# Softmax sums of an attention: folded by transfers through HBM in place of ones-matmuls on TensorE, with the additions around them moved

## The chip, the cores and the metric

One core of a Trainium2 chip. The metric is the device time of one execution in microseconds (us), as the median of the runs on a chip; a kernel before and a kernel after are always timed on the same chip, in turn. No run of this case has to be set aside as a slow one: the runs of each kernel lie within 0.6% of each other. The granted clock, the share of its full clock that the chip let TensorE have, is given where it matters.

## The reference, cut to what matters

```python
# x: (8, 512, 32, 32); 8 images, 256 channels inside, 4 heads of 64 channels, 1024 positions
x = x + block(_gn(x), ...)            # _gn: group norm over each image

def block(x, ...):
    t = cbs(x, cv1_w, cv1_bn, 0)      # 1x1 convolution, batch norm, SiLU ("cv1")
    ys = [t[:, :C], t[:, C:]]
    for i in range(2):                # two attentions per image
        yi = ys[-1]
        z = cbs(yi, m_cv1_w[i], m_cv1_bn[i], 1)              # 3x3 convolution
        z = bot_attention(z, m_qkv_w[i], m_rw[i], m_rh[i])
        z = silu(bn_eval(conv2d(z, m_cv2_w[i], 0), m_cv2_bn[i]))
        ys.append(yi + z)
    return cbs(concatenate(ys), cv2_w, cv2_bn, 0)

def bot_attention(x, qkv_w, rw, rh):
    q, k, v = ...                     # 1x1 convolution
    r = rw + rh                       # position term, the same for every image
    a = softmax(einsum('bhdi,bhdj->bhij', q, k + r) * 64 ** -0.5)
    return einsum('bhij,bhdj->bhdi', a, v)
```

## The kernel before: the parts that matter

An attention runs in four groups; a group is two heads by 512 queries. In a group TensorE goes through four pairs of key blocks: it makes the logits (`l_ps`), ScalarE takes their exponential into `pt`, VectorE adds the exponentials up in `acc`, and TensorE multiplies them with v into `av_ps`, one pair later. At a group's end ScalarE and VectorE evict `av_ps` (copy it out of PSUM, the memory in which this kernel has TensorE's results) into `ao`. There is a single `av_ps` tile, so the product with v of the next group waits for this eviction. The sum over the 128 partitions of `acc`, the softmax's denominator, comes one group later, and two groups later `ao` is scaled by its reciprocal `rs`.

```python
def add_up(pair):                                   # VectorE: 1.22 us each
    g, j0 = pair[0]
    pt = pts[pair[0]]
    if j0 == 0:
        accs[g] = act.tile([P, 2, HALF], F32, tag="acc", name="acc", bufs=2)
        return nc.vector.tensor_tensor(accs[g], pt[:, 0], pt[:, 1], ALU.add)
    for i in range(PAIR):
        ins = nc.vector.tensor_tensor(accs[g], accs[g], pt[:, i], ALU.add)
    return ins

def times_v(pair):
    ...                                             # matmuls into avs[g]
    if j0 + PAIR == NJ:
        av = avs.pop(g)
        dst = ao[:, c, ts(half, HALF)]
        nc.scalar.copy(dst, av[:, 0])
        evicted[0] = nc.vector.tensor_tensor(dst, av[:, 1], dst, ALU.add)

def sums(g):                                        # the sum over partitions, on TensorE
    NQ4 = HALF // 2
    ps = ps_big.tile([P, NQ4], F32, tag="big", name="s_ps")
    acc = accs.pop(g)
    for at_q in range(4):
        hd, part = divmod(at_q, 2)
        nc.tensor.matmul(ps[at_q * 32 : (at_q + 1) * 32, :], ones[:, 0:32],
                         acc[:, hd, ts(part, NQ4)], start=True, stop=True,
                         tile_position=(0, at_q * 32))
    ...                                             # ScalarE copies it, SP stores 4 rows to HBM

def spread(g, s_dram):                              # load them as 128x8, invert, spread again
    nc.vector.reciprocal(rc, total(g, s_dram))
    nc.sync.dma_start(r_dram.rearrange("h (i r) -> (h i) r", r=QP), rc)
    ...                                             # two loads that repeat a row give rs

for i in range(len(pairs) + 1):
    if i < len(pairs):
        added = logits(pairs[i])                    # l_ps, exponential, add_up
        g, at_q = divmod(i, NQ)                     # NQ = 4 pairs in a group
        with tc.issue_after(added.ins):
            if at_q == NQ - 2 and g > 0:            # behind the third pair's additions
                rss[g - 1] = spread(g - 1, s_drams[g - 1])
            if i == 1 and later is not None:
                later()                             # adds r to the second half of k
            if at_q == 1 and g > 1:
                scale(g - 2, rss.pop(g - 2))
    if i > 0:
        g, j0 = pairs[i - 1][0]
        if j0 == 0 and g > 0:
            s_drams[g - 1] = sums(g - 1)
        times_v(pairs[i - 1])
        ...
```

Other work is placed behind the attention's pairs: in the first attention of an image, the next image's group norm (`x<-x,gm,gr`, where `gr` is a small power on GpSimd) and the operands `t_x` of the next image's cv1, a Strassen product (fewer matrix products, for more additions before and after them); in the second, cv1's last additions and its own. The products of cv1 stand around the end of the first attention:

```python
def begin():
    for c in range(2):                              # VectorE: the operands t_x
        tt(t1[:, c], b12[c], b11[c], ALU.subtract)
        ...
    kept["ps"] = product(a11, b11)                  # x_ps; needs no t_x
    kept["m1"] = to(spare("xr", 2), kept["ps"])
    to(y0_2, product(s4, b22))                      # nor does this one
def rest():
    kept["m5"] = to(spare("xr", 2), product(s1, t1))
    ...
```

Of the kernel before, what the change touches and what calls it, by code (L numbers as in the profile page):

```python
# [59 lines left out]
def kernel(  # L62
# [170 lines left out]
    def make_sq(n, tag, bufs):  # L233
        (a11, a12), (a21, a22) = ([block_qkv(n, o, i) for i in range(2)] for o in range(2))
        parts = [act.tile([P, 2, 3, P], F32, tag=tag, name="sq_new", bufs=bufs) for _ in range(2)]
        s1, s2, s3, s4 = (t[:, j] for t in parts for j in range(2))
        nc.vector.tensor_tensor(s1, a21, a22, ALU.add)
        nc.vector.tensor_tensor(s2, s1, a11, ALU.subtract)
        nc.vector.tensor_tensor(s3, a11, a21, ALU.subtract)
        nc.vector.tensor_tensor(s4, a12, s2, ALU.subtract)  # L240
        for h, t in enumerate(parts):
            nc.gpsimd.dma_start(sq_dram[n][:, 2 * h : 2 * h + 2], t)

    def load_sq(n):
# [119 lines left out]
    def stages(act, small, ps_big, ps_av, n_pt):  # L364
# [245 lines left out]

        def project_strassen(n, z, sq, t):

# [90 lines left out]
            def later():  # L703
                for half in range(NH):
                    add_r(1, half)

            return q, kr, vT, later

        def attention_fast(n, z, at, behind, sq=None, t=None):



            q, kr, vT, later = (*project(n, z), None) if sq is None else project_strassen(n, z, sq, t)
            behind.get(-1, lambda: None)()

# [7 lines left out]
            def logits(pair):  # L723
# [15 lines left out]
                if pair is pairs[-1]:  # L739
                    with tc.issue_after(exp.ins):  # L740
                        silu_in.append(table_of(AF.Silu))
                if j0 == 0 and g == 1 and later is not None:
                    accs[g] = None
                    return exp
# [33 lines left out]
            def sums(g):  # L778
# [15 lines left out]
                return s_dram  # L794

            def last_sums(g):

# [22 lines left out]

            def total(g, s_dram):

                nc.sync.dma_start(sums_all[:, at + g, :], s_dram.rearrange("a (i r) -> (a i) r", r=QP))
                return sums_all[:, at + g, :]

            def spread(g, s_dram):

                rs = act.tile([P, HALF], F32, tag="rs", name="rs", bufs=2)
                rc = small.tile([P, QP], F32, tag="rc", name="rc", bufs=2)
                nc.vector.reciprocal(rc, total(g, s_dram))  # L830
                r_dram = tc.dram_tile([2, HALF], F32, name=f"r_dram{at + g}")
# [13 lines left out]


            NQ = NJ // PAIR
            s_drams, rss, evicted = {}, {}, [None]
            for i in range(len(pairs) + 1):
                if i < len(pairs):  # L850
                    added = logits(pairs[i])
                    g, at_q = divmod(i, NQ)
                    with tc.issue_after(added.ins):
                        if at_q == NQ - 2 and g > 0:
                            rss[g - 1] = spread(g - 1, s_drams[g - 1])
                        if i == 1 and later is not None:
                            later()
                        if at_q == 1 and g > 1:
                            scale(g - 2, rss.pop(g - 2))
                if i > 0:  # L860
                    g, j0 = pairs[i - 1][0]
                    if j0 == 0 and g > 0:
                        s_drams[g - 1] = sums(g - 1)
                    times_v(pairs[i - 1])
# [258 lines left out]
        def strassen_cv1(w, sw, xts, y0, y1):  # L1123
# [8 lines left out]
            kept = {}  # L1132

            def product(w, rhs, ps=None):
                onto = ps is not None
# [19 lines left out]
            def begin():  # L1155
                t = [act.tile([P, 2, NM, HALF], F32, tag=tag, name="t_x") for tag in ("q", "k")]
                kept["t"] = t1, t2, t3, t4 = [t[i][:, j] for i in range(2) for j in range(2)]
                for c in range(2):
                    tt(t1[:, c], b12[c], b11[c], ALU.subtract)
                    tt(t2[:, c], b22[c], t1[:, c], ALU.subtract)  # L1160
                    tt(t3[:, c], b22[c], b12[c], ALU.subtract)
                    tt(t4[:, c], t2[:, c], b21[c], ALU.subtract)
                kept["ps"] = product(a11, b11)
                kept["m1"] = to(spare("xr", 2), kept["ps"])
                to(y0_2, product(s4, b22))

# [5 lines left out]
            def rest():  # L1172
                t1, t2, t3, t4 = ([t[:, c] for c in range(2)] for t in kept["t"])
                kept["m5"] = to(spare("xr", 2), product(s1, t1))
                kept["m6"] = to(spare("x", NX), product(s2, t2))
                to(y1_2, product(s3, t3))
                to(y1_1, product(a22, t4))

            def add_y0():
                tt(kept["m1"], kept["m6"], kept["m1"], ALU.add)  # L1180
                tt(y0_2, y0_2, kept["m1"], ALU.add)
                tt(y0_2, y0_2, kept["m5"], ALU.add)

            def add_y1():
                tt(y1_2, y1_2, kept["m1"], ALU.add)
                tt(y1_1, y1_2, y1_1, ALU.subtract)
                tt(y1_2, y1_2, kept["m5"], ALU.add)
# [6 lines left out]

            return begin, go_on, rest, add_y0, add_y1, finish

# [128 lines left out]
    for b in range(B):  # L1325
# [87 lines left out]
        else:  # L1413
            behind[-1] = lambda: make(1, 0, range(PAIRS))
        ao, check = s.attention_fast(0, z, b * N * NM * NH, behind, sq.get(0), t)
        made = None
# [43 lines left out]
        def first():  # L1460
            if six:
                six[5]()
            if more:
# [16 lines left out]
        if six:  # L1480
            behind |= {(1, 1): six[3], (2, 1): six[4]}
        ao, check = s.attention_fast(1, z, (b * N + 1) * NM * NH, behind, sq.get(1), t)
        ylast = act.tile([P, NM, HW], F32, tag="v", name="ylast")
# [104 lines left out]
```

## Time and profile before

| | kernel before |
|---|---|
| median of 3 runs (lowest to highest) | 2314.30 us (2313.58 to 2314.46) |
| span and mean granted clock of the profiled run | 2311.5 us, 0.998 |
| TensorE (PE) busy, and idle within the span | 2286.2 us, 25.3 us |
| VectorE (DVE) busy | 1840.2 us |

The page's first section gives each engine's busy time; the prediction below shows its lines, the chain and the cadence. Here are two groups of instructions, by line, as the page's fifth section lists them: line, engine, operation, out<-in, sizes, count, then busy us and mean ns of one, then the idle time of the engine ahead of them and what ended it.

```profile
L768 PE MATMUL av_ps<-pt,vT 64*64 64x512 f32 x4096 | 486.4, 591 | 0.5 <-DVE ao L776 0.5
L551 DVE TENSOR_SCALAR x<-x,gm,gr 128x1024 f32<-128x1024 f32 x28 | 20.9, 808 | 8.1 <-POOL gr L516 8.1
```

TensorE waits for the eviction (`ao`) for 0.5 us in the whole execution, and VectorE for `gr` on GpSimd for 8.1 us. These two waits are worth remembering.

### The profile page before, as it was taken

The numbers are of one execution on the slowest core, as the hardware profiler recorded it, in microseconds if no ns is written. First come the engines' busy times: TensorE is split into PE (matmuls) and PEld (weight loads), VectorE is DVE, ScalarE is ACT, GpSimd is POOL, SyncE is SP. The second block draws the span as 40 slices with busy tenths as digits, with TensorE's granted clock in tenths as the row PEclk, the third lists the DMA queues.
The fourth block names the chain that finished last, engine by engine and source line by source line (L and its number), as shares of the span: only waits on it lengthen the run. The fifth ranks groups of instructions, "written<-read, shape, count | busy, mean of one in ns | idle before, by whom it ended". The sixth has DMA issues, their size and how long they took to land.

```text
span 2311.5 us, 36527 instructions
## 1 busy us (share of the span) xinstructions
PE 2286.2 (99%) x14806; PEld 1172.4 (51%) x14806; DVE 1840.2 (80%) x2920; ACT 987.6 (43%) x1292; POOL 89.1 (4%) x308
## 2 busy tenths in 40 slices
PE   7999999999999999999999999999999999999998
PEld 4546355463554636446364553646436364473643
DVE  8888878888788877887788887788877988777774
ACT  2443524435154452544525354253542525335352
POOL 1000000000000000000000000000000000000000
PEclk9999999999999999999999999999999999999999
DMA  7422333041430415213161221603116030260201
GB/s 239 174 86 87 120 134 154 16 151 34 174 118 26 136 48 202 76 53 108 52 240 37 76 87 47 250 29 102 59 47 250 29 133 29 75 221 16 87 11 62
DMA packets 95521, 235.60 MB, mean 102 GB/s; under 512 B 28016, under 2 KB 50736, under 8 KB 81904
## 3 DMA queue, kind: packets, MB, share of 16 engines
q1 hardware_dynamic: 83600, 182.84, 23.3%
q0 software_dynamic: 11744, 50.34, 5.7%
q8 instruction: 119, 1.95, 0.3%
q14 instruction: 58, 0.48, 0.1%
HBM read 198.54 MB, written 34.60 MB: 101 GB/s over the span
## 4 chain that ended last, share of the span: by engine, by line
PE 96%; DVE 3%; ACT 0%; DMA 0%; POOL 0%; issue 0%; SPq 0%; DVEq 0%; ACTq 0%
PE av_ps L768 19%; PE l_ps L734 19%; PE c_ps L970 14%; PE c L1028 8%; PE p_ps L630 8%; PE x_ps L1140 6%; PE c_new L1028 6%; PE m_ps L994 5%; PE ps L386 4%; PE pv_ps L634 3%; PE s_ps L786 1%; PE p_ps L634 1%; PE s_ps L804 1%; DVE acc L754 0%; PE v_ps L595 0%; DMA x<-in_x_dram 0%
## 5 line engine op out<-in xcount | busy, mean ns | idle before, releaser
L738 ACT ACTIVATE pt<-l_ps 128x1024 f32<-128x1024 f32 x512 | 494.8, 1023 | 410.1 <-PE l_ps L734 385.5
L754 DVE TENSOR_TENSOR acc<-acc,pt 128x1024 f32<-128x1024 f32 x384 | 469.5, 1223 | 65.5 <-ACT pt L738 40.0
L768 PE MATMUL av_ps<-pt,vT 64*64 64x512 f32 x4096 | 486.4, 591 | 0.5 <-DVE ao L776 0.5
L734 PE MATMUL l_ps<-q,kr 64*64 64x512 f32 x4096 | 485.9, 590 | 0.0
L970 PEld LDWEIGHTS c_ps<-v_in,u 128*128 128x128 f32 x2720 | 306.0, 192 | 6.7 <-issue 6.7
L970 PE MATMUL c_ps<-v_in,u 128*128 128x128 f32 x2720 | 306.1, 275 | 0.0
L768 PEld LDWEIGHTS av_ps<-pt,vT 64*64 64x64 f32 x4096 | 159.2, 133 | 269.4 <-issue 225.1
L734 PEld LDWEIGHTS l_ps<-q,kr 64*64 64x64 f32 x4096 | 160.0, 133 | 263.3 <-issue 252.2
L452 ACT COPY m<-c_ps 128x256 f32<-128x256 f32 x96 | 35.4, 369 | 216.3 <-PE c_ps L970 213.6
L1028 PE MATMUL c_new<-t_in,ws 128*128 128x512 f32 x288 | 124.6, 592 | 0.0
L994 PE MATMUL m_ps<-ao,m_sb 128*128 128x512 f32 x256 | 112.5, 592 | 0.0
L369 ACT ACTIVATE m_kept<-m_kept,bh,sh 128x512 f32<-128x512 f32 x42 | 31.9, 805 | 146.0 <-DVE m_kept L1112 86.3
L752 DVE TENSOR_TENSOR acc<-pt 128x1024 f32<-128x1024 f32 x64 | 78.1, 1220 | 18.0 <-ACT pt L738 18.0
L1028 PEld LDWEIGHTS c_new<-t_in,ws 128*128 128x128 f32 x288 | 54.7, 190 | 68.9 <-issue 66.0
L630 PE MATMUL p_ps<-t_z,sq 128*128 128x512 f32 x180 | 87.1, 593 | 0.0
L369 ACT ACTIVATE t<-m_ps,bh,sh 128x512 f32<-128x512 f32 x64 | 48.1, 776 | 83.9 <-PE m_ps L994 82.5
L994 PEld LDWEIGHTS m_ps<-ao,m_sb 128*128 128x128 f32 x256 | 48.6, 190 | 61.2 <-issue 61.0
L369 ACT ACTIVATE z<-z,bh,sh 128x512 f32<-128x512 f32 x64 | 48.6, 806 | 56.1 <-DVE z L481 56.1
L1002 DVE TENSOR_TENSOR ylast<-t,ypad 128x512 f32<-128x512 f32 x32 | 22.0, 692 | 63.2 <-ACT t L369 63.2
L445 DVE TENSOR_TENSOR v_in<-w_rows 128x512 f32<-128x512 f32 x96 | 65.6, 683 | 0.0
L453 DVE TENSOR_TENSOR r_mid<-c_ps,m 128x256 f32<-128x256 f32 x64 | 27.1, 423 | 46.5 <-ACT m L452 46.5
L1028 PE MATMUL c<-ypad,ws 128*128 128x512 f32 x144 | 63.8, 592 | 0.0
(255 smaller groups left out, 2997.3 us busy)
## 6 DMA issues: line engine op xcount, KB each, us to landing
u<-u SPq DMA_DIRECT2D x85, 1024.0 KB
x<-in_x_dram SPq DMA_DIRECT2D x32, 512.0 KB
x_res<-in_x_dram POOLq DMA_DIRECT2D x32, 512.0 KB, 6.9
out_dram<-m_kept POOLq DMA_DIRECT2D x28, 512.0 KB, 7.3
u<-u_new POOLq DMA_DIRECT2D x12, 1024.0 KB, 6.3
w<-in_cv_w_dram SPq DMA_DIRECT2D x12, 1024.0 KB
rs<-r_dram SPq DMA_DIRECT2D x96, 128.0 KB
ws<-s SPq DMA_DIRECT2D x24, 512.0 KB
```

What stands on the lines that cost most here:

```text
L369: return nc.scalar.activation(dst, src, AF.Silu, scale=sh[:, k : k + 1], bias=bh[:, k : k + 1])
L386: last_product[0] = nc.tensor.matmul(ps[:, half, :], w_of(k), rhs_of(k, half), start=(k == begin), stop=(k == end))
L630: nc.tensor.matmul(ps[:, o, :], w[:, o, :], rhs, start=not onto, stop=True, skip_group_check=onto)
L634: nc.tensor.matmul(v[:, ts(j, P)], rhs[:, ts(j, P)], w[:, 2, :], start=j == 0 and not onto, stop=True, skip_group_check=True,)
L734: nc.tensor.matmul(ps[kh * HD : (kh + 1) * HD, hd, :], kr[r, c, o : o + HD], q[r, c, ts(half, HALF)], start=True, stop=True,)
L738: exp = nc.scalar.activation(pt[:, i], ps, AF.Exp, scale=SCALE)
L754: ins = nc.vector.tensor_tensor(accs[g], accs[g], pt[:, i], ALU.add)
L768: nc.tensor.matmul(avs[g][hd * HD : (hd + 1) * HD, kh, :], vT[r, j, o : o + HD], pt[r, i, hd, :], start=(j == 0), stop=(j == NJ - 1),)
L970: nc.tensor.matmul(ps[:, row, col, :], us[i][:, k, row, SLOT[col], :], vs[i][:, k, row, col, :], start=(k == 0), stop=(k == NM - 1),)
L994: nc.tensor.matmul(pss[oc][:, half, :], m2_sb[:, n, k, ts(oc, P)], ao[:, k, ts(half, HALF)], start=(k == 0), stop=(k == NM - 1),)
L1028: nc.tensor.matmul(ps[:, o, :], w[:, k, ts(o, P)], rhs[part][:, c, :], start=(k == 0 and not onto), stop=(k == KB - 1), skip_group_check=onto,
L1140: nc.tensor.matmul(ps[:, o, :], w[:, c, ts(o, P)], rhs[c], start=(c == 0 and not onto), stop=(c == 1), skip_group_check=onto,)
```

## The change

Its intent: TensorE makes up nearly the whole chain, so take the ones-matmul off it. The four quarters of `acc`'s partitions go to HBM; two of them are loaded, the other two are added onto them by an accumulating transfer from GpSimd; VectorE adds the remaining two, transposes in blocks of 32 and reduces. Image 0 keeps the matmuls. To make room, the first addition of each group goes behind the eviction, r is added by an accumulating transfer from a table, and cv1's order is changed so that two of its sums form in PSUM, which spares VectorE one addition.

```diff
+            def fold(g):
+                acc = accs.pop(g).rearrange("p h (a q) -> p (h a) q", a=2)
+                NQ4 = HALF // 2
+                f_dram = tc.dram_tile([2, 2, 4, 32, NQ4], F32, name=f"f_dram{at + g}")
+                for s in range(4):
+                    nc.sync.dma_start(f_dram[s % 2, s // 2].rearrange("a k q -> k a q"), acc[s * 32 : (s + 1) * 32])
+                parts = act.tile([P, 2, NQ4], F32, tag="h", name="fold", bufs=2)
+                nc.sync.dma_start(parts, f_dram[0].rearrange("s a k q -> (a k) s q"))
+                nc.gpsimd.dma_start(parts, f_dram[1].rearrange("s a k q -> (a k) s q"), accum_op=ALU.add)
+                return parts
...
-            def total(g, s_dram):
+            def total(g, parts):
+                if not folded:
+                    ...
+                a, b = parts[:, 0], parts[:, 1]
+                nc.vector.tensor_tensor(a, a, b, ALU.add)
+                flipped = b.rearrange("p (r k) -> p r k", k=32)
+                nc.vector.transpose(flipped, a.rearrange("p (i r) -> p r i", r=QP))
+                nc.vector.tensor_reduce(sums_all[:, at + g, :], flipped, AX.X, ALU.add)
                 return sums_all[:, at + g, :]
...
-                if j0 == 0 and g == 1 and later is not None:
+                if j0 == 0 and (g > 0 if folded else g == 1 and later is not None):
                     accs[g] = None          # first addition: behind the eviction
...
-                        s_drams[g - 1] = sums(g - 1)
+                        folds[g - 1] = fold(g - 1) if folded else sums(g - 1)
...                                          # r, from image 2 on
+                nc.gpsimd.dma_start(kr[:, 1, :], r_dram, accum_op=ALU.add)
...                                          # cv1, begin()
-                to(y0_2, product(s4, b22))
+                kept["ps5"] = product(s1, [t1[:, c] for c in range(2)])
+                kept["m5"] = to(spare("xr", 2), kept["ps5"])
...                                          # cv1, rest()
-                kept["m5"] = to(spare("xr", 2), product(s1, t1))
+                to(y0_2, product(s4, b22, kept["ps5"]))
```

The place of `spread`, behind the third pair's additions of the next group, is unchanged. With the fold it is there, in the order of VectorE's program, that it meets the end of the path through HBM.

More of the change, by code (lines that the diff above doesn't have):

```diff
@@ L242, in make_sq, with make_r @@
             nc.gpsimd.dma_start(sq_dram[n][:, 2 * h : 2 * h + 2], t)
+    r_dram = [tc.dram_tile([P, HW], F32, name=f"r{n}") for n in range(N)]
+    def make_r(n):
+        r = act.tile([P, F, F], F32, tag="xr", name="r_new", bufs=2)
+        nc.vector.tensor_tensor(
+            r, rw_sb[:, n, 1, :].unsqueeze(1).to_broadcast([P, F, F]),
+            rh_sb[:, n, 1, :].unsqueeze(2).to_broadcast([P, F, F]), ALU.add,
+        )
+        nc.gpsimd.dma_start(r_dram[n], r.rearrange("p a b -> p (a b)"))
     def load_sq(n):
@@ L609, in first_sum, with project_strassen @@
             return t
-        def project_strassen(n, z, sq, t):
+        def project_strassen(n, z, sq, t, r_dram=None):
             q = act.tile([P, NM, HW], F32, tag="q", name="q")
@@ L703, in later, with attention_fast @@
             def later():
-                for half in range(NH):
-                    add_r(1, half)
+                if r_dram is None:
+                    for half in range(NH):
+                        add_r(1, half)
+            if r_dram is not None:
+                nc.gpsimd.dma_start(kr[:, 1, :], r_dram, accum_op=ALU.add)
             return q, kr, vT, later
-        def attention_fast(n, z, at, behind, sq=None, t=None):
-            q, kr, vT, later = (*project(n, z), None) if sq is None else project_strassen(n, z, sq, t)
+        def attention_fast(n, z, at, behind, sq=None, t=None, r_dram=None, folded=False):
+            q, kr, vT, later = (*project(n, z), None) if sq is None else project_strassen(n, z, sq, t, r_dram)
             behind.get(-1, lambda: None)()
@@ L819, in last_total, with spread @@
                 nc.vector.tensor_tensor(sums_all[:, at + g, :], cs[:, 0], cs[:, 1], ALU.add)
-            def total(g, s_dram):
-                nc.sync.dma_start(sums_all[:, at + g, :], s_dram.rearrange("a (i r) -> (a i) r", r=QP))
+            def total(g, parts):
+                if not folded:
+                    nc.sync.dma_start(sums_all[:, at + g, :], parts.rearrange("a (i r) -> (a i) r", r=QP))
+                    return sums_all[:, at + g, :]
+                a, b = parts[:, 0], parts[:, 1]
[3 more added lines that the diff above has]
+                nc.vector.tensor_reduce(sums_all[:, at + g, :], flipped, AX.X, ALU.add)
                 return sums_all[:, at + g, :]
-            def spread(g, s_dram):
+            def spread(g, parts):
                 rs = act.tile([P, HALF], F32, tag="rs", name="rs", bufs=2)
                 rc = small.tile([P, QP], F32, tag="rc", name="rc", bufs=2)
-                nc.vector.reciprocal(rc, total(g, s_dram))
+                nc.vector.reciprocal(rc, total(g, parts))
                 r_dram = tc.dram_tile([2, HALF], F32, name=f"r_dram{at + g}")
@@ L847, in attention_fast @@
             NQ = NJ // PAIR
-            s_drams, rss, evicted = {}, {}, [None]
+            folds, rss, evicted = {}, {}, [None]
             for i in range(len(pairs) + 1):
@@ L854, in attention_fast @@
                         if at_q == NQ - 2 and g > 0:
-                            rss[g - 1] = spread(g - 1, s_drams[g - 1])
+                            rss[g - 1] = spread(g - 1, folds.pop(g - 1))
                         if i == 1 and later is not None:
@@ L1161, in begin @@
                     tt(t3[:, c], b22[c], b12[c], ALU.subtract)
-                    tt(t4[:, c], t2[:, c], b21[c], ALU.subtract)
+                    tt(t4[:, c], b21[c], t2[:, c], ALU.subtract)
                 kept["ps"] = product(a11, b11)
                 kept["m1"] = to(spare("xr", 2), kept["ps"])
-                to(y0_2, product(s4, b22))
+                kept["ps5"] = product(s1, [t1[:, c] for c in range(2)])
+                kept["m5"] = to(spare("xr", 2), kept["ps5"])
             def go_on():
@@ L1172, in rest @@
             def rest():
-                t1, t2, t3, t4 = ([t[:, c] for c in range(2)] for t in kept["t"])
-                kept["m5"] = to(spare("xr", 2), product(s1, t1))
+                _, t2, t3, t4 = ([t[:, c] for c in range(2)] for t in kept["t"])
+                to(y0_2, product(s4, b22, kept["ps5"]))
                 kept["m6"] = to(spare("x", NX), product(s2, t2))
-                to(y1_2, product(s3, t3))
-                to(y1_1, product(a22, t4))
+                ps = product(s3, t3)
+                to(y1_2, ps)
+                to(y1_1, product(a22, t4, ps))
             def add_y0():
@@ L1181, in add_y0, with add_m5 @@
                 tt(y0_2, y0_2, kept["m1"], ALU.add)
-                tt(y0_2, y0_2, kept["m5"], ALU.add)
             def add_y1():
                 tt(y1_2, y1_2, kept["m1"], ALU.add)
-                tt(y1_1, y1_2, y1_1, ALU.subtract)
+                tt(y1_1, y1_1, kept["m1"], ALU.add)
+            def add_m5():
                 tt(y1_2, y1_2, kept["m5"], ALU.add)
@@ L1193, in finish @@
                             silu(dst[:, oc, :], dst[:, oc, :], bn + oc)
-            return begin, go_on, rest, add_y0, add_y1, finish
+            return begin, go_on, rest, add_y0, add_y1, add_m5, finish
         def cv2_part(w2, ys, oc, ks=range(2 * NM)):
@@ L1414 @@
             behind[-1] = lambda: make(1, 0, range(PAIRS))
-        ao, check = s.attention_fast(0, z, b * N * NM * NH, behind, sq.get(0), t)
+        if b == 1:
+            behind |= {(NG - 1, n + 1): lambda n=n: make_r(n) for n in range(N)}
+        ao, check = s.attention_fast(0, z, b * N * NM * NH, behind, sq.get(0), t, r_dram[0] if b > 1 else None, b > 0)
         made = None
@@ L1461, in first @@
             if six:
-                six[5]()
+                six[6]()
             if more:
@@ L1480 @@
         if six:
-            behind |= {(1, 1): six[3], (2, 1): six[4]}
-        ao, check = s.attention_fast(1, z, (b * N + 1) * NM * NH, behind, sq.get(1), t)
+            behind |= {(1, 1): six[3], (2, 1): six[4], (3, 1): six[5]}
+        ao, check = s.attention_fast(1, z, (b * N + 1) * NM * NH, behind, sq.get(1), t, r_dram[1] if b > 1 else None, b > 0)
         ylast = act.tile([P, NM, HW], F32, tag="v", name="ylast")
```

## The prediction

> **What bounds the kernel now.** I read the page first, from its busy shares to its chain, then the chain in order of time over one attention, then the VectorE's timeline over the same stretch. The span is 2311.5 us; TensorE is busy for 99% of it and makes up nearly all of the chain that ended last.
>
> ```profile
> PE 2286.2 (99%) x14806; PEld 1172.4 (51%) x14806; DVE 1840.2 (80%) x2920; ACT 987.6 (43%) x1292; POOL 89.1 (4%) x308
> ...
> PE 96%; DVE 3%; ACT 0%; DMA 0%; POOL 0%; issue 0%; SPq 0%; DVEq 0%; ACTq 0%
> ```
>
> The groups by line show the instructions that the change takes away: 48 sums of 8 records each.
>
> ```profile
> L786 PE MATMUL s_ps<-acc,ones 128*32 128x256 f32 x384 | 30.7, 391 | 0.0
> ```
>
> A busy TensorE could still be slow, so I looked at the cadence, in the chain of waits around the first attention of image 3 (start, length, what):
>
> ```profile
> 959.88 1.72 PE l_ps L734 x16
> 961.60 0.57 PE s_ps L786 x8
> 962.17 1.88 PE av_ps L768 x16
> 964.05 1.72 PE l_ps L734 x16
> ```
>
> Every stretch of 16 records takes 1.72 us, one after the other, at a granted clock of 1.00. So TensorE has no slack in the attention: only fewer instructions, or a new wait, can move the time. One sum over the softmax terms (s_ps) costs its own 0.57 us, and the stretch behind it takes 1.88 in place of 1.72: together **0.73 us**. That agrees with the distance of two groups' starts, 14.46 us (962.17 to 976.63), against eight stretches of 1.72, 13.73.
>
> VectorE stands second, at 80% over the span but more in the attentions. From its timeline, the end of the same attention:
>
> ```profile
> 995.29 2.98 DVE L551 TENSOR_SCALAR x<-x,gm,gr 128x1024 f32<-128x1024 f32 x4 [1.16 <-POOL gr L516]
> 998.20 2.55 DVE L754 TENSOR_TENSOR acc<-acc,pt 128x1024 f32<-128x1024 f32 x2
> 1000.66 0.20 DVE L830 RECIPROCAL rc<-sums_all 128x8 f32<-128x8 f32 x1
> 1000.85 2.56 DVE L754 TENSOR_TENSOR acc<-acc,pt 128x1024 f32<-128x1024 f32 x2
> 1003.32 0.68 DVE L1159 TENSOR_TENSOR t_x<-x 128x512 f32<-128x512 f32 x1
> ```
>
> TensorE finishes this attention at 1001.79, so VectorE is already 1.5 us behind when it starts the operands t_x of the next image's first convolution. Today that is harmless: the two Strassen products put there (x times a11, x times s4) need no t_x. In groups 1 to 3 of this attention VectorE's free time is only about 0.6 us at two places in each of two groups, plus the 1.16 us above.
>
> [...] s_ps is in 128x32 tiles between 64x64 ones, streams a quarter of the columns of 16 av_ps records (0.43 us by that ratio), yet costs 0.73. [...] No run before has an accumulating one; plain ones from GpSimd land 2.3 us (256 KB) to 6.9 us (512 KB) after issue. [...]
>
> **The change, part by part.**
> 1. *Removed from TensorE*: 3 sums in each of 14 attentions (images 1 to 7), 42 x 0.73 = **30.7 us**, all on the chain. ScalarE loses 42 copies of 0.38 us, off the chain.
> 2. *In its place, the fold*: four stores of 128 KB to HBM, a 256 KB load, a 256 KB accumulating load from GpSimd, then on VectorE an addition (128x256, 0.42 us by the rows of that size), a 32x32 transposition [...] and a reduction (0.42), each waiting for the one before. With a gap of about 0.05 each that is an estimated 1.6 us of VectorE per group. For the path I put the stores at 3.5 us (four issues of 0.4 to 0.5, then some 1.5 as r_dram's store takes from issue to the next issue: 970.73 to 972.17), the load at 2.5, the accumulation at 3: an estimate of **9 us**, 8 to 11.
> 3. *Removed from VectorE*: four additions of r (0.69 each, 2.5 us) at the start of 12 attentions, now an accumulating transfer of 512 KB needed 27 us later (hidden); one addition of 1.2 us per cv1. Neither frees time where it is short, which is groups 1 to 3 of the first attention.
> 4. *Moved*: the first addition of a group goes behind the eviction of av_ps, so the eviction waits 1.2 us less. It is needed: without s_ps TensorE gets to av_ps 0.57 us earlier, and the eviction is done only 0.4 us (962.10 - 961.67) to 0.8 us before it does today.
> 5. *Moved*: in cv1 the product s1 times t1 now stands second, ahead of s4; t1 comes from VectorE. The instruction order shows too that GpSimd's rstd of the group norm (gr) now stands behind the third accumulating transfer.
>
> *First attention of images 1 to 6*, in the times of image 3. VectorE's work per group from eviction to eviction, summed from the timeline plus 1.6: group 1 is 12.2 + 1.6 = 13.8; group 2 (a scaling, small operations more) 15.2; group 3 (with the norm's application and its wait) 15.9. TensorE needs 13.73. Group 1's eviction can start at 960.6, so group 2's starts at 974.4, group 3's at 989.6, and t_x at 1005.5. TensorE: group 3's av_ps is held by about 1.0 us; its product with a11 then starts at 1001.79 - 3 x 0.73 + 1.0 = 1000.6 and ends at 1004.1. t1's first half is there at 1006.2 (2.1 us of waiting), its second at 1008.0, wanted at 1007.1 (0.9 more). gr comes later than now by an estimated 0.7: GpSimd cannot go on before the stores and the load (6 us behind 988.9) and its own issue of 0.73. Sum 1.0 + 3.0 + 0.7 = 4.7 us, against the gain of 2.2. Six times: 28.2. Image 1 still adds r itself and makes r's table (two of 1.2 us in group 3): 2.4 more.
>
> *Second attention of images 1 to 6*: VectorE has room, but the path of 9 us starts when a group's last addition ends and must end behind the third pair's additions of the next: about 9.2 us in group 1, 7.6 in group 2. So group 2 waits about 1.4 us, 0.6 of it is slack at the eviction, 0.8 reaches TensorE: 4.8. Image 7 has neither norm nor cv1: its gain stays whole.
>
> Sum: -30.7 + 28.2 + 2.4 + 4.8 = **+4.7 us**, or 2319. The shorter end of the fold's operations (1.3 us) would take 2 to 3 us off, so I say **2317**.
>
> **The rivals.**
> (a) *TensorE's saving comes through whole*: 2314.3 - 30.7 = 2284. For it: the chain is TensorE alone. Against: 13.8 to 15.9 us of VectorE work in groups of 13.73. Should the fold's operations hide in gaps and t1 be ready, 2290 to 2300 is the result.
> (b) *VectorE becomes the bound in the first attentions*, as worked out above: 2310 to 2325.
> (c) *The path through HBM is the new wait*: at 11 us or more it holds VectorE in every group of both attentions, the eviction with it: 2 to 3 us more in each of some 12 attentions, 2335 to 2350. For it: three dependent transfers in place of two small ones, on DMA engines that also carry 1 MB weight loads. Against: those engines are at 7% and 15% in these two attentions.
> (d) *The 512 KB of r come late*: unlikely, it has 27 us.
>
> **Range and chances.** The two large terms pull against each other: 30.7 is sure to 2 us, the 35 of waits only to about half. (a) at its best and (c) at its mildest give the range of 2293 to 2338. Being 2% faster needs 2268, more than all of TensorE's saving; 2% slower needs 2361, beyond the whole of (c). So: faster 0.02, same 0.94, slower 0.04.
>
> **What would show it.** s_ps of 128x32 falls from 384 records to 48, and groups without stalls are 13.7 us apart. In the first attentions, TensorE should wait before av_ps of the last group for ao, and above all before the second x_ps product for t_x, 2 to 4 us; VectorE has next to no idle time there. gr should wait on GpSimd. In the second attentions the fold's addition should show a wait for the accumulating transfer of 0 to 3 us. Adding the three operations should give about 1.6 us; if they and the waits are well under that, (a) is right. I am wrong if t_x is there in time, or if the accumulating transfer takes 5 us or more by itself.

## The result and the profile after

| | before | after |
|---|---|---|
| median (lowest to highest) | 2314.38 us (2313.58 to 2314.55) | 2449.82 us (2445.12 to 2453.52) |
| ratio of fast runs | | 1.0586, 95% interval 1.057 to 1.0601 |
| span and granted clock of the profiled run | 2311.5 us, 0.998 | 2443.7 us, 0.975 |
| PE busy, idle | 2286.2, 25.3 us | 2315.2, 128.5 us |

Ratios, here and below, are the mean time of one kernel's fast runs over that of the other's in the same rounds, so not quite the ratio of the medians quoted. The changed kernel is 5.9% slower, outside the predicted range. All four of its runs lie within 0.4%, so this is no slow state.

The page of the kernel after, its busy times and its chain:

```profile
PE 2315.2 (95%) x14470; PEld 1175.8 (48%) x14470; DVE 1862.9 (76%) x2994; ACT 978.4 (40%) x1250; POOL 151.5 (6%) x364
...
PE 56%; DMA 9%; DVE 7%; issue 2%; ACT 1%; SPq 0%; POOL 0%; POOLq 0%; DVEq 0%
```

TensorE has 336 records fewer and is busy for longer, and its share of the chain has fallen from 96% to 56%. Two things happened then: TensorE waits (103 us more idle time), and the same work takes longer on it. The groups that answer to those of before, and the fold's first addition (line numbers have moved: L768 is L784 now, L551 is L564):

```profile
L784 PE MATMUL av_ps<-pt,vT 64*64 64x512 f32 x4096 | 503.6, 610 | 45.0 <-DVE ao L792 44.7
...
L857 DVE TENSOR_TENSOR fold<-fold 128x256 f32<-128x256 f32 x42 | 17.8, 424 | 97.0 <-DMA fold<-f_dram 97.0
```

The wait for the eviction went from 0.5 to 45.0 us, and VectorE sits 97.0 us in front of the fold's addition, waiting for its transfer. The list of waits (who waits for whom: us in total, times, longest) shows the rest of TensorE's:

```profile
DVE x L564 <- POOL gr L529: 24.0, 7, 4.6
...
PE l_ps L750 <- DVE gm L518: 21.2, 6, 4.4
...
PE x_ps L1177 <- DVE t_x L1196: 19.4, 9, 4.4
...
PE c L1064 <- DVE ao L792: 18.6, 7, 4.2
```

TensorE's waits for av_ps, gm, t_x and c add up to 103.9 us, all for VectorE. (The convolution c waits for `ao` because it uses the one av tile.) VectorE's wait for gr went from 8.1 to 24.0 us, and its wait for `rs`, which comes out of the fold and two more transfers, from 9.0 to 24.0.

The chain of waits in order of time over a group of image 3's first attention (start, length, what) shows the path of one fold from end to end:

```profile
1021.42 1.23 DVE acc L770
...
1023.92 2.89 DMA f_dram<-acc
...
1026.88 2.80 DMA fold<-f_dram
...
1030.36 4.57 DMA fold<-f_dram
...
1034.96 0.43 DVE fold L857
...
1046.83 0.09 POOL fold L822
...
1047.54 0.61 POOL w_rows L430
...
1048.19 0.98 POOL gr L529
1049.17 0.03 issue
1049.19 0.04 DVE x L564
```

`acc` is complete at 1022.65. The four stores are issued from 1022.82 and the last lands at 1026.81; the load takes 2.80; GpSimd takes 0.68 to come to its transfer; the accumulation takes 4.57, and at 1034.96 VectorE can add. That is **12.3 us**. Over all 42 folds of this execution the same distance is 11.9 us in the median, 10.4 to 13.6. The last lines show the next group: GpSimd comes to gr only behind the next accumulating transfer, and VectorE waits for it. VectorE's timeline over that stretch (the bracket is its idle time before, and what ended it):

```profile
1034.96 0.42 DVE L857 TENSOR_TENSOR fold<-fold 128x256 f32<-128x256 f32 x1 [2.10 <-DMA fold<-f_dram]
1035.42 0.64 DVE L859 STREAM_TRANSPOSE fold<-fold 128x256 f32<-128x256 f32 x1
...
1049.19 2.98 DVE L564 TENSOR_SCALAR x<-x,gm,gr 128x1024 f32<-128x1024 f32 x4 [3.87 <-POOL gr L529]
```

The last line answers to the one at 995.29 of before, where the same wait for gr was 1.16 us.

TensorE's timeline in the second attention of that image, and the granted clock in three stretches of it (the stretch, its length, then the engines' busy times, the clock, and DMA's share and GB/s):

```profile
1164.78 1.95 PE L784 MATMUL av_ps<-pt,vT 64*64 64x512 f32 x16 [1.30 <-DVE ao L792]
...
1182.78 3.15 PE L784 MATMUL av_ps<-pt,vT 64*64 64x512 f32 x16 [4.04 <-DVE ao L792]
1185.69 2.46 PE L750 MATMUL l_ps<-q,kr 64*64 64x512 f32 x16
```

```profile
1177.00:1182.00 5.00, 1.74 (x20) 0.31 (x8) 4.86 (x7) 2.53 (x3) 0.74 (x1) 1.00 0.23 45
1182.80:1186.00 3.20, 3.20 (x20) 1.14 (x24) 2.99 (x3) 0.00 (x0) 0.00 (x0) 0.59 0.83 246
1187.90:1191.00 3.10, 3.10 (x36) 1.09 (x32) 2.45 (x2) 1.56 (x3) 1.01 (x3) 1.00 0.26 77
```

Behind a wait of 1.30 us the 16 products take their usual time; behind 4.04 us they take 3.15, the granted clock is 0.59 there, and some 5 us after the restart it is 1.00 again.

Where the span went can be read from the attentions' lengths, from the first `l_ps` to the first `m_ps`, the product of `ao` with m_cv2's weights (other products stand in between), all 16 of an execution, from TensorE's timeline: their sum is 1132.1 us before and 1262.9 after, so the attentions hold 130.8 of the 132.2 us. In the mean of images 2 to 6:

| | before | after |
|---|---|---|
| first attention | 69.1 us | 77.8 us |
| second attention | 72.3 us | 82.5 us |

Image 1's grew most (84.6 and 88.0 us); those of image 7 by 2.5 to 2.8; those of image 0, which keeps the matmuls, by 0.3 at most.

### The profile page after: what moved, and what is told of

The parts are those of the page before. It is cut to its first block, busy times and chain, and to the rows that moved or that the text cites. A ratio compares the mean times of both kernels' runs of the same rounds, so it can differ in the third digit from the quotient of the medians.

```text
span 2443.7 us, 36273 instructions
## 1 busy us (share of the span) xinstructions
PE 2315.2 (95%) x14470; PEld 1175.8 (48%) x14470; DVE 1862.9 (76%) x2994; ACT 978.4 (40%) x1250; POOL 151.5 (6%) x364
## 4 chain that ended last, share of the span: by engine, by line
PE 56%; DMA 9%; DVE 7%; issue 2%; ACT 1%; SPq 0%; POOL 0%; POOLq 0%; DVEq 0%
PE c_ps L1006 11%; PE l_ps L750 8%; PE av_ps L784 7%; DMA fold<-f_dram 6%; PE c L1064 6%; PE p_ps L643 6%; PE c_new L1064 5%; PE x_ps L1177 5%; PE m_ps L1030 4%; DVE acc L770 3%; PE ps L399 2%; PE pv_ps L647 2%; DMA f_dram<-acc 2%; PE p_ps L647 1%; ACT pt L754 1%
## 5 line engine op out<-in xcount | busy, mean ns | idle before, releaser
L784 PE MATMUL av_ps<-pt,vT 64*64 64x512 f32 x4096 | 503.6, 610 | 45.0 <-DVE ao L792 44.7
L750 PE MATMUL l_ps<-q,kr 64*64 64x512 f32 x4096 | 500.1, 606 | 21.2 <-DVE gm L518 21.2
L784 PEld LDWEIGHTS av_ps<-pt,vT 64*64 64x64 f32 x4096 | 163.2, 137 | 339.2 <-issue 229.6
L822 POOL DMA_DIRECT2D fold<-f_dram x42 | 50.4, 1201 | 773.0 <-ACT pt L754 405.8
L1177 PE MATMUL x_ps<-t_x,sw 128*128 128x512 f32 x144 | 76.7, 686 | 19.4 <-DVE t_x L1196 19.4
L857 DVE TENSOR_TENSOR fold<-fold 128x256 f32<-128x256 f32 x42 | 17.8, 424 | 97.0 <-DMA fold<-f_dram 97.0
L1064 PEld LDWEIGHTS c_new<-t_in,ws 128*128 128x128 f32 x288 | 54.7, 190 | 68.9 <-issue 66.0
L768 DVE TENSOR_TENSOR acc<-pt 128x1024 f32<-128x1024 f32 x64 | 77.9, 1217 | 5.1 <-ACT pt L754 5.1
```

The costliest lines, as they stand in the source:

```text
L750: nc.tensor.matmul(ps[kh * HD : (kh + 1) * HD, hd, :], kr[r, c, o : o + HD], q[r, c, ts(half, HALF)], start=True, stop=True,)
L784: nc.tensor.matmul(avs[g][hd * HD : (hd + 1) * HD, kh, :], vT[r, j, o : o + HD], pt[r, i, hd, :], start=(j == 0), stop=(j == NJ - 1),)
L1064: nc.tensor.matmul(ps[:, o, :], w[:, k, ts(o, P)], rhs[part][:, c, :], start=(k == 0 and not onto), stop=(k == KB - 1), skip_group_check=onto,
L1177: nc.tensor.matmul(ps[:, o, :], w[:, c, ts(o, P)], rhs[c], start=(c == 0 and not onto), stop=(c == 1), skip_group_check=onto,)
```

## The experiments

The theory after the result: the wait for the fold's path, 12.3 us long and in a loop with the next group's additions, is the loss. The rivals: VectorE's own work in the fold; the other two parts (r by transfer, cv1's order); GpSimd, held up by accumulating transfers; the added HBM traffic. Eleven kernels were run. Their diffs are against the kernel after unless said otherwise. A kernel that is wrong on purpose is marked so; its relative error was 0.142.

### e1_no_fold: everything but the fold

```diff
-        ao, check = s.attention_fast(0, ..., r_dram[0] if b > 1 else None, b > 0)
+        ao, check = s.attention_fast(0, ..., r_dram[0] if b > 1 else None, False)
```

and the same in the second attention: the matmul sums are back, r by transfer and cv1's new order stay.

> The changed kernel with the fold undone in every attention (sums again by TensorE, first additions in their old place); r by transfer and the new order of cv1's products stay. Theory A (the path of the fold through HBM, 12.3 us in the trace, holds VectorE's queue) and theory B (the fold's three VectorE operations, 1.7 us per group, are too much work for VectorE) both expect 2300 to 2325 us. Theory C (the other parts, cv1's order above all, cost the time) expects over 2400 us.

Measured: 2319.10 us against 2313.52, ratio 1.0024 (1.0007 to 1.004), correct. r and cv1's order cannot be the cause by themselves: of some 135 us they make 5.6.

### e2_no_wait: the fold's work without its wait (wrong on purpose)

```diff
-                a, b = parts[:, 0], parts[:, 1]
-                nc.vector.tensor_tensor(a, a, b, ALU.add)
+                x = act.tile([P, 2, HALF // 2], F32, tag="wt", name="idle", bufs=2)
+                a, b = x[:, 0], x[:, 1]
+                nc.vector.tensor_tensor(a, forty, forty, ALU.add)
```

All transfers and VectorE operations stay, but the operations work on a constant and wait for no transfer.

> The changed kernel, but VectorE's three fold operations read a constant instead of what the transfers bring: same work, same traffic, no wait for it (the result is wrong on purpose). Theory A expects 2295 to 2340 us, with next to no waiting at av_ps in the second attentions; what is left over 2284 is VectorE's load in the first attentions. Theory B expects 2420 us or more, as the work is all there. A theory D (the added traffic itself slows other transfers or engines) expects over 2400 too.

Measured: 2351.22 us, ratio 1.0175 (1.0147 to 1.0203), clock 0.990. 98.6 us of the loss are gone with the wait; but 37.7 remain, above the 2340 to which the expectation reached. Of the waits, TensorE's for `ao` at av_ps has gone to 0.5 us, as before the change; these remain:

```profile
DVE x L566 <- POOL gr L531: 29.3, 7, 5.2
PE x_ps L1180 <- DVE t_x L1199: 29.2, 6, 7.2
```

So there is a second cause, and gr on GpSimd is the suspect.

### e3_late: the fold's results taken one pair later

```diff
-                        if at_q == NQ - 2 and g > 0:
+                        if at_q == NQ - (1 if folded else 2) and g > 0:
                             rss[g - 1] = spread(g - 1, folds.pop(g - 1))
...
-                        if at_q == 1 and g > 1:
+                        if at_q == (2 if folded else 1) and g > 1:
                             scale(g - 2, rss.pop(g - 2))
```

The path gets 3.4 us more before VectorE asks for its result.

> The changed kernel with the fold's VectorE operations one pair later in the queue (behind the fourth pair's additions of a group in place of the third's, scaling one pair later too): same work, same transfers, about 4 us more time for the path. Theory A expects 2295 to 2350 us: a path of 12.3 us against some 13 us then available. Theory B expects no gain, 2420 us or more.

Measured: 2351.36 us, ratio 1.0165 (1.0148 to 1.0182), correct, just above the expected range: as fast as the kernel that does not wait at all. (That they are equal is in part chance: in images 2 to 6 its first attentions take 1.3 us more than e2's, its second ones 1.4 us less.) Its waits:

```profile
PE x_ps L1177 <- DVE t_x L1196: 31.5, 12, 6.1
...
DVE x L564 <- POOL gr L529: 29.3, 7, 6.2
...
DVE fold L857 <- DMA fold<-f_dram: 11.9, 14, 2.0
...
PE av_ps L784 <- DVE ao L792: 3.4, 8, 0.9
```

The fold's wait fell from 97.0 to 11.9 us, and TensorE's at av_ps from 44.7 to 3.4. VectorE's wait for `rs` rose, from 24.0 to 51.3 us, but behind it TensorE hardly waits. This shows the path's length against the place where it is asked for, with a right result. The wait for gr is the one that e2 has.

### e4_load2: a plain load and an addition in place of the accumulating transfer

```diff
-                nc.gpsimd.dma_start(parts, f_dram[1].rearrange("s a k q -> (a k) s q"), accum_op=ALU.add)
+                    nc.sync.dma_start(t, f_dram[n].rearrange("s a k q -> (a k) s q"))   # n = 0, 1: two tiles
...
+                nc.vector.tensor_tensor(parts[0], parts[0], parts[1], ALU.add)
```

> The changed kernel with the accumulating load replaced by a second plain load from the sync queue and one more VectorE addition (128x512, 0.69 us per group, 42 times 29 us of VectorE work more): the path gets shorter by the accumulation's 4.6 us and GpSimd's 0.7 us before it, to 7 to 8 us. Theory A expects 2310 to 2360 us. Theory B expects it slower than the changed kernel, 2450 to 2480 us.

Measured: 2376.49 us, ratio 1.0282 (1.0264 to 1.0299), correct: far below the kernel after, but above the 2360 to which theory A reached, so the expectation was missed. Two of VectorE's waits:

```profile
DVE fold L858 <- DMA fold<-f_dram: 16.8, 12, 3.5
...
DVE x L564 <- POOL gr L529: 8.1, 7, 1.2
```

The fold's wait is 16.8 us and the wait for gr is back at 8.1, its value before the change. So the accumulating transfer costs twice: by its own length, 4.3 us in the median of the kernel after, and by what stands behind it on GpSimd, where the wait for gr is 24.0 us in the kernel after and 8.1 here. This kernel still is slower than e3, with 26 us more VectorE work than the kernel after (1889.3 against 1862.9 us busy).

### e5_work_only: as e2, and no transfers of the fold (wrong on purpose)

> As e2_no_wait, and the fold's transfers are left out altogether: VectorE's three operations on a constant stay, nothing is stored, loaded or accumulated (result wrong on purpose). e2 left 2351 us. Theory E (in the first attentions GpSimd's rstd of the group norm, gr, stands behind the third accumulating transfer and comes late) expects gr on time and a fall to 2310 to 2332 us, with the first attentions at 71 to 73 us in place of 75.6. Theory F (VectorE's load alone makes e2's rest) expects 2345 to 2355 us, first attentions still at 75 to 76.

Measured: 2319.38 us against 2313.53, ratio 1.0025 (1.001 to 1.0041). The wait for gr is 8.1 us. So the 31.8 us from here to e2 belong to the transfers that nobody waits for: either to their traffic or to GpSimd. e11 tells these apart. TensorE's timeline shows two waits for t_x in each first attention: 1.0 and 0.68 us in images 2 to 6, 3.13 and 0.68 in image 1.

### e6_work_old_cv1: as e5, with cv1's old order (wrong on purpose)

> As e5_work_only, with cv1's products and sums in their old order (s4 times b22 second, t1 needed only behind m2). If the early need of t1 costs what the prediction worked out (3 us per first attention of images 1 to 6, 18 us in all), this is 12 to 22 us below e5_work_only and the waits for t_x are gone. If VectorE's delay just comes out at m2 instead, it is within 5 us of e5_work_only.

Measured: 2302.90 us, ratio 0.9954 (0.9939 to 0.9969). With VectorE's fold work in place of the sums (and r by transfer and the moved additions), 10.6 of the 30.7 us come through. Of the 20 that are lost, TensorE's waits show about 13: 7.7 us for gm, in six waits, and 6.0 at av_ps, in 13, where the kernel before has none and 0.5. The rest stays open. Against e5, cv1's new order costs 16.5 us: t1 comes from a VectorE that is late by the fold's work.

### e11_no_wait_sp: as e2, the accumulating transfer replaced by a plain one from SP (wrong on purpose)

```diff
-                nc.gpsimd.dma_start(parts, f_dram[1].rearrange("s a k q -> (a k) s q"), accum_op=ALU.add)
+                nc.sync.dma_start(parts, f_dram[1].rearrange("s a k q -> (a k) s q"))
```

> As e2_no_wait (2351 us), with the accumulating transfer replaced by a plain one of the same size from the sync queue, which nothing waits for: the traffic stays, GpSimd has no transfer ahead of gr. Theory E (gr late behind the accumulating transfer makes the step from e5's 2319 to e2's 2351) expects 2318 to 2330 us and VectorE's wait for gr back at about 1 to 2 us. If the traffic itself makes the step, it stays at 2340 to 2355.

Measured: 2318.40 us against 2314.13, ratio 1.0019 (1.0004 to 1.0034). The waits for gr and t_x:

```profile
PE x_ps L1180 <- DVE t_x L1199: 11.9, 12, 3.3
...
DVE x L566 <- POOL gr L531: 8.3, 7, 1.3
```

The same stores, and as many loads, cost nothing against e5 as long as none stands on GpSimd ahead of gr. So the rival of HBM traffic falls, and the second cause is GpSimd's order: it comes to gr only behind an accumulating transfer that itself waits for the stores and the load (29.3 us of waiting for gr in e2, 8.3 here).

### e8_first_adds: e3, with the first additions back ahead of the eviction

```diff
-                if j0 == 0 and (g > 0 if folded else g == 1 and later is not None):
+                if j0 == 0 and g == 1 and later is not None:
```

> As e3_late, with the groups' first additions in their old place, ahead of the eviction. If the eviction is as short of time as worked out (without the sum TensorE comes to av_ps 0.57 us earlier, and an addition of 1.2 us ahead of the eviction is then in the way), 0.3 to 1.2 us of waiting in each of 42 groups: 2362 to 2400 us, the waits of av_ps for ao well above e3_late's 35 us. If the move does nothing here, 2345 to 2357 us.

Measured: 2366.97 us against 2313.53, ratio 1.0234 (1.0218 to 1.0249), correct; 15.6 us slower than e3 (of another chip). TensorE's wait for `ao` at av_ps is 26.5 us:

```profile
PE av_ps L784 <- DVE ao L792: 26.5, 25, 1.9
```

In e3 it is 3.4 us. The "35 us" of the expectation is a misreading: it is the sum of e3's waits at av_ps and at x_ps (3.4 and 31.5). This part of the change does what it was made for.

### e10_fold_alone: before, with the fold and the moved additions only

The diff is long but simple: r is added by VectorE and cv1 has its old order, all else as in the kernel after.

> The fold and the moved first additions alone, on the kernel before: r is added by VectorE, cv1 is as before. Theory A (the fold's path holds VectorE, other parts matter little) expects 2425 to 2480 us, about what the whole change takes. If the whole change is slow only through the parts together, this is under 2400.

Measured: 2439.27 us against 2314.13, ratio 1.0539 (1.0523 to 1.0555), correct. With e1 this closes the ring: the fold (with the moved additions) brings nearly the whole loss, the rest without it almost none.

### e7_second_late: the fold only where there is room, late; no r table, old cv1

The fold stands in the second attentions of images 1 to 7 and in image 7's first, one pair later as in e3.

> A version meant to beat both: the fold only in the second attentions of images 1 to 7 and the first of image 7, with its VectorE operations one pair later as in e3_late; the first attentions of images 1 to 6 keep TensorE's sums, r is added by VectorE, cv1 is as before. From e3_late's times of the attentions (70.5 against 72.3 us, and 66.7 against 68.9 in image 7): 6 x 1.8 + 2 x 2.2 = 15 us less than before, so 2296 to 2302 us. If the gain in e3_late's second attentions came from the other parts (r by transfer, cv1), it stays at 2308 or more.

Measured in 5 rounds: 2316.89 us against 2313.53, ratio 1.0016 (1.0003 to 1.003), correct. The 2296 to 2302 that it was made for was missed. Its second attentions take 73.5 us, more than the 72.3 of before:

```profile
PE av_ps L784 <- DVE ao L792: 15.5, 13, 1.6
DVE fold L857 <- DMA fold<-f_dram: 15.2, 9, 3.1
```

VectorE is short there: this kernel has the additions of r and of cv1 back, and the evictions come late.

### e9_second_late_cv1: the same, with cv1's new order and r by transfer in second attentions

```diff
-        ao, check = s.attention_fast(0, ..., r_dram[0] if b > 1 else None, b > 0)
+        ao, check = s.attention_fast(0, ..., None, not more)
...
+        if b == 1:
+            behind[NG - 1, 2] = lambda: make_r(1)
```

with the later places of e3. (`not more` is the last image.)

> A second try to beat both kernels: as e7_second_late (fold only in the second attentions of images 1 to 7 and the first of image 7, one pair later), but with cv1's new order and sums, and with r by transfer in the second attentions from image 2 on (its table is made in the second attention of image 1). e7 kept 73.5 us per second attention, with waits at av_ps in groups where cv1's additions stand; e3_late with one addition fewer had 70.5. If VectorE's load in those groups made e7's loss, the second attentions come to 70.5 to 71 us and the whole to 2299 to 2308 us. If e3_late's 70.5 needed something else, it stays at 2312 or more.

Measured in 5 rounds: **2302.95 us** (2302.66 to 2303.44) against 2314.13, ratio 0.9951 (0.9937 to 0.9964), correct. It beats both kernels: by 0.5% that of before, clear of the noise since the whole interval lies below 1, and by 6% that of after. Second attentions take 70.6 to 70.7 us in images 2 to 6. In e1, with the same order of cv1 and r by transfer but without the fold and its moved additions, they take 72.3, so the fold itself brings the 1.7 us there. After image 0, TensorE's timeline shows only two waits over 0.3 us, 0.78 and 0.34 at av_ps. The page:

```profile
PE 2273.8 (99%) x14614; PEld 1169.4 (51%) x14614; DVE 1854.2 (81%) x2963; ACT 981.4 (43%) x1268; POOL 124.2 (5%) x339
```

So the change's other two parts together make the room that the fold needs (13.9 us between e7 and e9), and the fold pays here where its path and GpSimd's order are out of the way.

## Why the prediction was wrong

**The account by differences**, between the medians above (of several chips, whose medians of the kernel before lie within 0.9 us): before 2313.5; VectorE's fold work in place of the sums, with r by transfer and the moved additions, 2302.9 (e6, -10.6); cv1's new order 2319.4 (e5, +16.5); the accumulating transfers on GpSimd 2351.2 (e2, +31.8); the wait for the path 2449.8 (+98.6). The order of the steps matters: in the first attentions the wait for gr and that for the path lie side by side, so the last step is smaller there than the path alone would make it. In images 2 to 6, first attentions go from 75.3 us (e2, mean) to 77.8, second ones from 72.1 to 82.5; over images 1 to 7 the first grow by 23.0 us and the second by 72.7. So most of those 98.6 us were lost in the second attentions, of each of which the prediction let 0.8 us reach TensorE.

**The step that failed is the path**, an estimate of "9 us", "8 to 11". It measured 12.3 in the group shown and 11.9 in the median. By terms, in that group: the stores 4.0 with 0.2 ahead, where I put 3.5; the load 2.8 for 2.5; the accumulation 4.6 for 3, its median over 42 transfers 4.3 (the 3 was my estimate; the kernel before has no accumulating transfer to show it); and 0.7 of GpSimd's own waits and issue, which I had left out. Rival (c) had the mechanism, and "at 11 us or more" was its condition; so the mechanism was named and its size was off. (The plain GpSimd transfers that the prediction listed for comparison were not all: among those of 512 KB in the kernel before, medians go from 3.3 to 7.3 us.)

**The path was set against a gap and not against a loop.** I asked whether 9 us fit between a group's last addition and the third pair's additions of the next, and found 1.4 us missing in one group. But a late fold makes the fourth pair's additions late, these end the next group's `acc`, and from there the next path starts. The loop is 12.3 us of path, 1.7 of the fold's operations (0.42, 0.64, 0.42 and a reciprocal of 0.20) and 2.5 of additions: an estimate of 16.5 us per group, from the durations above. In the trace `acc` ends at 1022.65 and again at 1039.17, 16.5 us later; in the second attention of the image the same distances are 17.1 and 18.0. TensorE needs 13.73. So a group can lose 2.8 us or more, in both attentions; VectorE waited for the fold in 31 of 42 groups, 27.7 us in first attentions, for which the prediction counted nothing, and 69.3 in second ones. This made (c) worth much more than the "2 to 3 us more in each of some 12 attentions" that I gave it. e3 confirms the loop from the other side: 3.4 us more room takes 85 of the 97 us of waiting away, and the fourth pair's additions, now ahead of the fold, no longer wait for it in the same turn.

**The clock was missed altogether.** Nothing in the prediction says that TensorE is slower behind a wait. The trace of the kernel after shows it for long waits: clock 0.59 behind the wait of 4.04 us, 1.00 some 5 us later; the slowest stretches of 16 products take 3.69 us against the usual 1.90. What it is worth can be read from two kernels with the same 14470 TensorE records: e11, with few waits, is busy for 2264.8 us on TensorE, the kernel after for 2315.2. Its page:

```profile
PE 2264.8 (98%) x14470; PEld 1165.8 (50%) x14470; DVE 1860.8 (80%) x2994; ACT 976.6 (42%) x1250; POOL 101.1 (4%) x323
```

So of the 127.6 us between their spans 50.4 are slower matmuls and 77.2 are idle time: two fifths were no waiting at all. Busy time multiplied by the mean granted clock is 2258 us in e11 (0.997) and 2257 in the kernel after (0.975), so the lower clock is the whole of the slower matmuls. No run changes the clock alone, so that the lower clock follows from the waits is read from the timelines and not shown by an experiment.

**gr was under-sized**, "later than now by an estimated 0.7". The reasoning, GpSimd behind the third accumulating transfer, was right and e11 and e4 show it. But in e2 and e3 VectorE waits 29.3 us for gr in 7 waits, against 8.1: 3.0 us more each time. The chain above shows the terms: `acc` ends at 1039.17 and GpSimd comes to its transfer at 1046.83, 7.7 us later, where I put 6; from there to the end of gr it is 2.3 us (the issue, two memsets that are caught behind it, then gr), where I put 0.73 for the issue and gr takes 1.03 today. Then the lateness goes on to t_x and x_ps, and the clock is charged on top: of the 31.0 us between the spans of e5 and e2, 21.0 are TensorE's idle time, as much as the wait for gr grew (21.2), and 10.0 longer busy time at a clock of 0.990 in place of 0.996.

**What was right.** A sum costs 0.73 us: in e2 image 7's attentions fall from 68.9 to 66.7 us, three times 0.73. The fold's operations take 1.55 us with gaps, from 1034.96 to 1036.51 (1.6 estimated; the transposition's part of that was my estimate, shown by no trace then, and it took 0.64). cv1's new order waits for t1, with 1.7 us in five of the six first attentions of e5 and 3.8 in the other, where I put 3.0. r by transfer is hidden: no instruction in the kernel after waits for the accumulation onto k (making the table in image 1 holds ScalarE once, for 5.1 us). The first additions behind the eviction are needed (e8).

**The chances** of 0.04 for slower came from "beyond the whole of (c)", 2350. I had named "if the accumulating transfer takes 5 us or more by itself" as what would make me wrong; it took 4.3, and I was wrong already, for a loop has no tolerance once it is longer than the engine's own cycle, here 16.5 us against 13.73.

**What stays open.** Why some waits of 1.9 to 2.9 us are followed by slow matmuls and others of that length are not; how the 98.6 us divide between the first and the second attentions without gr's wait beside it; and what the fold would be worth in every attention with both cures at once, the later place of e3 and the plain load of e4, which no run has.

## What to carry to other kernels

Before moving work from the bounding engine to a chain of dependent transfers, write down the loop that it closes (last input, path, the operations behind it, the next input) and compare that with the engine's cycle; here a path that nearly fitted made VectorE wait in 31 of 42 groups. Ask for the result as late as the schedule allows: here one pair later, and the fold only where VectorE had room and no GpSimd work stood behind it, made a loss of 5.9% into a gain of 0.5%. In a kernel like this one count a wait of TensorE as more than itself: here 77.2 us of idle time came with 50.4 us of slower matmuls.

## What the traces show of these transfers, waits and operations

- An accumulating transfer from GpSimd, in the kernel after: 256 KB take 4.3 us from issue to landing (3.9 to 4.7, 42 transfers), 512 KB 5.3 (5.1 to 5.6, 12 transfers). The issue holds GpSimd for 1.20 and 0.93 us; that of a plain transfer from GpSimd takes 0.53 to 0.73 in the mean of its group.
- Store, load and accumulating load in a row: 11.9 us in the median (10.4 to 13.6, 42 times) for 512 KB stored and 256 KB twice loaded.
- GpSimd's next operations behind such an issue: in the group shown gr ends 2.3 us after the issue begins. The spans of the operations behind it are longer (a memset 0.61 us against 0.13, gr 1.51 against 1.03 in the median), but they overlap with the issue and with each other; gr's own part, from the end of the memsets, is 0.98 us, so that it is slower in itself is not shown.
- Matmuls behind a wait, in the kernel after, in stretches of 16 `av_ps` or `l_ps` products: all 11 that came behind 3.08 to 4.73 us took 2.93 to 3.69 us, against the usual 1.90; all 6 behind 0.33 to 1.65 us took 1.95. In between it is mixed: 3.13 us after a wait of 1.92 and 3.30 after 2.82, but 1.95 after 2.23. The cost, 50 us or 2% of the span, came with 37 waits of 0.3 to 4.7 us behind image 0.
- A 32x32 block transposition with a strided source: 0.64 us for 128x256 in fp32 (42 times), against 0.42 for a dense addition of that size.
